# Cross-attention over 64 batches: who makes the output's last step, when x is turned, and the order of both ends

## The chip, the cores and the metric

One core of a Trainium2 chip runs the whole kernel in one launch. The metric is the time of the launch on the device in microseconds (us), as the median of several runs; lower is better. The times of one profiled execution are also used, and they are said to be so.

## What is computed

There are 64 batches. In each, `x` is 256 x 512 and `ctx` 256 x 384, all float32:

```python
text_p  = x   @ W_text  + b_text          # 256 x 512
audio_p = ctx @ W_audio + b_audio         # 256 x 512
Q = layer_norm(text_p,  g1, beta1)
K = layer_norm(audio_p, g2, beta2)
alpha = softmax(Q @ K.T / sqrt(512))      # 256 x 256
H = (alpha @ audio_p) @ W_out + b_out
out = layer_norm(H + x, g_out, beta_out)
```

The last layer norm is, for each row y: subtract the mean, multiply by `g_out` (the "shift"), multiply by the row's 1/sqrt(var + eps), and add `beta_out`. The last two are "the output's last step" below.

## The kernel before, in words

A batch's 256 rows are two tiles of 128 partitions. The instructions of every engine run in the order in which the program writes them down (`tc.manual_schedule()`): no planner moves them, and an instruction that waits holds everything behind it on its engine. Waits between engines come from the tile framework, by the tiles that are read and written. "Turning" is VectorE's 32 x 32 block transpose; rows go to DRAM and come back in blocks of 32 rows (`store`, `fetch`) so that a turn gives a full transpose.

The three products with weights are made with fewer multiplications than usual, by sums of blocks. `Thirds` does k (from ctx, object `k2`) and the output (object `o`, with W_audio and W_out folded into `wao`); its block sums `csum` and `zsum` are seven GpSimd additions each (`Sides.add`). Its products fall into steps `one` to `five` on TensorE in the PSUM places M (`ps_m`), L (`ps_l`), T and U (`ps_u`), N (`ps_n`). Between the steps stand VectorE instructions that read and rewrite PSUM: `after_one` (a copy of N1, then T = N0 - N1), `after_three` (a copy of T, then L0 = M0 + t and L1 = M1 - t), `after_four` (two), and ScalarE/VectorE copies `after_five`, `leave`, `leave_plus`. `Fork` does q from x in two PSUM banks (`ps_f`); its block sums `xsum` are four GpSimd additions, and its VectorE steps are `after_six` (two) and `after_five` (one).

The main loop runs over b from 0 to 61 and is a pipeline. One iteration, "batch b" below, holds: k and q of batch b+2 (`k2`, `q2`); the scores and the softmax of b (`at`); the context product of b-1 (`last`); the output product of b-2 (`old`); and the last layer norm of b-3 (`settled`). The turns in it are `turn_c(b+3)`, `q[b+1].turn()`, `k[b+1].turn([0])` and `([1])`, `turn_x(b+3)`, and `turn_e` of b-1. The layer norm of `settled` is: `sums` and `deviations` on ScalarE (L782, L790), 1/sqrt on GpSimd (L372 and L376, tile `rstd`), and on VectorE `shift` for both tiles (L897) and `settle` for both (L906):

```python
    def settle(self, t):
        nc.vector.scalar_tensor_tensor(
            self.y[:, t, :], self.y[:, t, :], self.r[t], beo_sb, ALU.mult, ALU.add
        )
```

`settle(0)` stands in batch b behind `shift(1)`; `settle(1)` stands in the next iteration, followed by the store of both tiles on SyncE's queue. What follows the loop (batches 61 to 63: `old`, `last`, `at`, `end`) is written out by hand, as is everything ahead of it, where weights are centred, folded and summed.

Of the kernel before, what the change touches and what calls it, by code (L numbers as in the profile page):

```python
# [11 lines left out]
ALU = mybir.AluOpType  # L12
# [10 lines left out]
def kernel(  # L23
# [18 lines left out]
    nc = tc.nc  # L42
# [171 lines left out]
    def bias_parts():  # L214

        part = once.tile([P, D], F32, tag="e", name="part")
        nc.vector.tensor_scalar(part, wo_sb[:, 0, :], bac_sb[:, 0:1], None, ALU.mult)
        for k in range(1, HC):
            nc.vector.scalar_tensor_tensor(
                part, wo_sb[:, k, :], bac_sb[:, k : k + 1], part, ALU.mult, ALU.add  # L220
            )

        nc.vector.tensor_tensor(part[:1], part[:1], bo_sb, ALU.add)
        return part

    wao_sb = const.tile([P, AC, D], F32, tag="wao", name="wao")
    bao_sb = const.tile([P, D], F32, tag="bao", name="bao")
# [54 lines left out]
    def sum_x(xT):  # L282

        n = DC // 2
        part = lambda i, j: xT[:, j * n : (j + 1) * n, bass.ts(i, P)]
        s = work.tile([P, 4, n, P], F32, tag="xsum", name="xsum")
        add = nc.gpsimd.tensor_tensor
        add(s[:, 0], part(1, 0), part(1, 1), ALU.add)
        add(s[:, 1], s[:, 0], part(0, 0), ALU.subtract)
        add(s[:, 2], part(0, 0), part(1, 0), ALU.subtract)  # L290
        add(s[:, 3], part(0, 1), s[:, 1], ALU.subtract)
        ss = {
            1: part(0, 0), 2: part(0, 1), 4: part(1, 1),
            5: s[:, 0], 6: s[:, 1], 7: s[:, 2], 3: s[:, 3],
        }
        return {p: [ap[:, k, :] for k in range(n)] for p, ap in ss.items()}
# [357 lines left out]
    class Attention:  # L654
# [252 lines left out]
                self.y[:, t, :], self.y[:, t, :], self.r[t], beo_sb, ALU.mult, ALU.add  # L907
            )

        def finish(self, lo=0, n=LT):  # L910
            for t in range(lo, lo + n):
                self.shift(t)
                self.settle(t)

        def store(self, lo=0, n=LT):
            nc.sync.dma_start(
# [4 lines left out]
    def turn_x(b):  # L921
        xT = work.tile([P, DC, L], F32, tag="xT", name=f"xT_{b}")
        turn(xT, blocks[b][1], DC)
        return xT

    def turn_c(b):
        cT = work.tile([P, AC, S], F32, tag="cT", name=f"cT_{b}")
        turn(cT, blocks[b][0], AC)
        return cT
# [91 lines left out]
    k[0].turn()  # L1021
    k[0].affine(g2_sb, be2_sb)
    part = bias_parts()
    wa_t = const.tile([P, 11, W3], F32, tag="wa_thirds", name="wa_thirds")
    wa_blocks = third_weights(wa_sb, wa_t, [0])
    fold_multiply(2, 0, 2)
    q[1].six()
    q[1].after_six()
    q[0].turn()
    cT[2] = turn_c(2)  # L1030
    cs[2] = Sides(cT.pop(2), "csum").add()
    fold_multiply(2, 2, 4)
# [2 lines left out]
    q[1].five()  # L1035
    q[1].after_five()
    xT[2] = turn_x(2)
    xs[2] = sum_x(xT.pop(2))
    third_weights(wa_sb, wa_t, [1], nc.vector)
    fold_bias(part)  # L1040
    q[1].rest()
    q[1].square()
    q[1].scales()
    ba_delta = third_bias(ba_sb, "ba_delta")
    bao_delta = third_bias(bao_sb, "bao_delta")
    Thirds.seed_with(ba_sb)
# [13 lines left out]
    for b in range(B - 2):  # L1060
        at = att[b] = att.get(b) or Attention(b)
        settled, old, last = att.pop(b - 3, None), att.get(b - 2), att.get(b - 1)
        three = b + 3 < B
        if b + 4 < B and b != 1:
            load_c(b + 4)
            load_x(b + 4)
        if b == 2:
            go_sb = row(g_out, "go")
            beo_sb = row(beta_out, "beo")
        if b == 0:  # L1070
            at.score(0, 8)
            Fork.seed()
        k2 = k[b + 2] = Thirds("k", b + 2, cs.pop(b + 2), wa_blocks, ba_sb, ba_delta)
        if b < 3:
            q[b + 2] = Fork(b + 2, xs.pop(b + 2), wt_blocks)
        q2 = q[b + 2]
        if settled:
            settled.sums()
        k2.one()
        k2.after_one()  # L1080
        if b < 2:
            Fork.clear()
        if b == 1:
            last.reciprocals()
            last.divide_e()
            last.store_e()
            load_c(b + 4)
            last.fetch_e()
            load_c_rows(b)
            load_x(b + 4)  # L1090
        k2.two()
        if old:
            old.context_two(0)
            old.context_two(1)
            old.copy_two()
        k2.three()
        if three:
            cT[b + 3] = turn_c(b + 3)
        if b:
            at.affine_keys(0, 1)  # L1100
        k2.after_three()
        if old:
            old.start_products()
        if b < 3:
            q2.one()
            q2.after_one()
        q2.seven()
        q2.after_seven()
        if b:
            at.affine_keys(2, 3)  # L1110
        if done:
            done.settle(1)
            done.store()
        done = settled
        if b > 1:
            last.fetch_e()
            load_c_rows(b)
            load_x_rows(b - 1)
        if not three:
            last_rows(B - 2)  # L1120
            last_rows(B - 1)
        q2.six()
        q2.after_six()
        if settled:
            settled.deviations()
        if three:
            cs[b + 3] = Sides(cT.pop(b + 3), "csum").add(2 if b > 1 else 5)
        k2.four()
        k2.after_four()
        if settled:  # L1130
            settled.shift(0)
        q2.five()
        q2.after_five()
        if settled:
            settled.shift(1)
            settled.settle(0)
        if b:
            at.affine_queries(0, 1)
        k2.five()
        k2.after_five()  # L1140
        k2.leave()
        k2.last_middle()
        if three:
            cs[b + 3].add(3 if b > 1 else 0)
        if old:
            old.o.seed()
        elif three:
            k2.seed()
        if b:
            at.affine_queries(2, 3)  # L1150
        q2.rest()
        q2.square()
        q2.scales()
        q[b + 1].turn()
        k[b + 1].turn([0])
        k2.square()
        k2.scales()
        if b:
            at.score(0, 2)
        if old:  # L1160
            old.o.one()
            old.o.after_one()
            old.o.two()
        if three:
            xT[b + 3] = turn_x(b + 3)
        if b:
            at.score(2, 4)
        if old:
            old.o.three()
            old.o.after_three()  # L1170
        k[b + 1].turn([1])
        if b:
            at.score(4, 7)
        if not three:
            att[b + 1] = Attention(b + 1)
            att[b + 1].affine_queries()
        q2.normalise()
        q2.store()
        if old:
            old.o.four()  # L1180
            old.o.after_four()
        if last:
            last.turn_e()
        if b:
            at.score(7, 8)
        if old:
            old.o.five()
        if three:
            Fork.seed()
        k2.normalise()  # L1190
        k2.store()
        q2.fetch()
        k2.fetch()
        if three:
            cs[b + 3].add()
            xs[b + 3] = sum_x(xT.pop(b + 3))
        if b < 2:
            wao_blocks = third_weights(wao_sb, wao_t, [b])
        at.maxima()
        if three and b:  # L1200
            Fork.clear()
        if not three:
            att[b + 1].affine_keys()
        at.exponentials()
        if three and b > 1:
            q3 = q[b + 3] = Fork(b + 3, xs.pop(b + 3), wt_blocks)
            q3.one()
            q3.after_one()
        if old:
            old.o.leave_plus(x_rows[b - 2], at.reciprocals)  # L1210
        elif b:
            at.reciprocals()
        if last:
            last.context_one()
        if three and old:
            k2.seed()
        if b:
            at.divide_e()
        if three and b:
            at.store_e()  # L1220
        if last:
            last.copy_one()

    settled, old, last = att[B - 5], att[B - 4], att[B - 3]
    at = att[B - 2]
    load_x_rows(B - 3)
    done.settle(1)
    done.store()
    for t in range(ST):
        old.context_two(t)  # L1230
# [17 lines left out]
    old.o.three()  # L1248
    old.o.after_three()
    k[B - 1].turn()  # L1250
    q[B - 1].turn()
    for t in range(ST):
        last.context_two(t)
    last.copy_two()
# [2 lines left out]
    k[B - 1].affine(g2_sb, be2_sb)  # L1257
    last.start_products()
    old.o.four()
    settled.settle(0)  # L1260
    old.o.after_four()
    settled.settle(1)
    settled.store()
    old.o.five()
# [15 lines left out]
    end.score(0, 8)  # L1280
    old.shift(0)
    old.shift(1)
    at.evict(0)
    at.scales(0, 1)
    last.o.four()
    last.o.after_four()
    end.maxima()
    end.exponentials()
    old.settle(0)
    old.settle(1)  # L1290
    old.store()
# [2 lines left out]
    at.settle(0)  # L1294
    last.o.five()
    last.o.leave_plus(x_rows[B - 3], lambda: None)
    at.multiply(1, bank[4])
    at.evict(1)
    at.scale_soon(1)
    end.transpose_e(bank[5])  # L1300
    end.copy_e()
    last.statistics()
    end.context()
    at.shift(1)
    at.settle_beside(1)
    at.store()
# [50 lines left out]
```

## Time and profile before

| | |
|---|---|
| median of 3 runs | 1411.28 us (1408.72 to 1413.8) |
| the profiled execution's own time | 1412.36 us |
| its span, first to last instruction | 1410.6 us |
| busy: TensorE, its weight loads | 98%, 88% |
| busy: VectorE, ScalarE, GpSimd | 87%, 78%, 72% |
| mean granted TensorE clock | 0.995 |
| one iteration of the loop in its middle | 21.2 us |

Engines are named PE (TensorE), PEld (its weight loads), DVE (VectorE), ACT (ScalarE), POOL (GpSimd) and SP (SyncE, which issues the DMAs). A timeline line gives the start in us from the first instruction, the duration, the engine, the line in the source, the operation, out<-in by tile names, the shape, how many instructions were merged, and in brackets how long the engine had been idle and what ended that. A matmul is recorded twice, and its end is modelled, so the distance from one start to the next is the better measure of what a matmul costs.

### The profile page before, as it was taken

Reading aid. Unit: us, or ns where it says so; the run is one execution under the profiler, and the core shown is the slowest. Engines: PE = TensorE matmul, PEld = TensorE weight load, DVE = VectorE, ACT = ScalarE, POOL = GpSimd, SP = SyncE. Lnnn points to the kernel's source line nnn. Section 1 sums busy time; section 2 is a strip of 40 time slices with the busy share of each in tenths; the row PEclk is TensorE's granted clock in tenths of the full one; section 3 lists DMA queues with packets and bytes.
Section 4 is the critical chain, followed back from the end, with each engine's and each line's share of the span. In section 5 each row is a group of like instructions: output and inputs, shape, how many; then the busy total and the mean of one; then the engine's idle time right before and its main releaser. Section 6 shows DMA issues by size and latency. Waiting matters only on the chain.

```text
span 1410.6 us, 26095 instructions
## 1 busy us (share of the span) xinstructions
PE 1388.2 (98%) x7423; PEld 1241.4 (88%) x7423; DVE 1225.0 (87%) x2559; ACT 1094.5 (78%) x2815; POOL 1017.5 (72%) x1685
## 2 busy tenths in 40 slices
PE   9899999999999999999999999999999999999996
PEld 5689999999999999999999999999999999999874
DVE  5768988988988988888988989988988988988877
ACT  4678878878878877877877878877877877877873
POOL 4787777777777777777777777787787687687644
PEclk9999999999999999999999999999999999999999
DMA  9688878778777878788778788887877778788661
GB/s 219 168 245 239 233 232 245 224 243 242 225 241 237 235 235 246 222 241 239 229 242 244 228 234 245 230 235 231 239 240 230 244 235 241 231 233 237 207 204 62
DMA packets 449095, 322.00 MB, mean 228 GB/s; under 512 B 153782, under 2 KB 381622, under 8 KB 448951
## 3 DMA queue, kind: packets, MB, share of 16 engines
q1 hardware_dynamic: 448854, 320.20, 77.9%
q8 instruction: 60, 0.98, 0.3%
q14 instruction: 85, 0.69, 0.2%
q10 hardware_dynamic: 96, 0.13, 0.0%
HBM read 203.57 MB, written 116.65 MB: 227 GB/s over the span
## 4 chain that ended last, share of the span: by engine, by line
PE 91%; DVE 2%; ACT 2%; POOL 2%; issue 1%; DMA 1%; SPq 1%; DVEq 0%; ACTq 0%; POOLq 0%
PE ps_f L603 26%; PE ps_m L502 16%; PE ps_sc L672 14%; PE ps_z L738 11%; PE ps_n L502 10%; PE ps_u L502 7%; PE ps_l L502 5%; SPq L72 1%; POOL csum L320 0%; DMA eq<-ed 0%; PE ps_f L392 0%; ACT qr L652 0%; POOL zsum L320 0%; PE ps_m L807 0%; ACT qT L477 0%
## 5 line engine op out<-in xcount | busy, mean ns | idle before, releaser
L320 POOL TENSOR_TENSOR zsum<-zT 128x256 f32<-128x256 f32 x124 | 73.6, 594 | 271.4 <-ACT zT L756 264.6
L672 PE MATMUL ps_sc<-kT,qT 128*128 128x256 f32 x1024 | 262.6, 381 | 0.5 <-ACT zT L753 0.5
L320 POOL TENSOR_TENSOR zsum<-zsum,zT 128x256 f32<-128x256 f32 x310 | 215.8, 714 | 14.6
L672 PEld LDWEIGHTS ps_sc<-kT,qT 128*128 128x128 f32 x1024 | 187.6, 191 | 18.5 <-ACT zT L753 0.9
L320 POOL TENSOR_TENSOR csum<-csum,cT 128x256 f32<-128x256 f32 x310 | 192.0, 628 | 10.0
L603 PE MATMUL ps_f<-wtsum,xsum 128*128 128x256 f32 x756 | 189.9, 387 | 1.7 <-DVE ps_f L486 1.4
L906 DVE SCALAR_TENSOR_TENSOR yr<-yr,rstd,beo 128x512 f32<-128x512 f32 x124 | 144.1, 1163 | 51.8 <-POOL rstd L376 51.8
L738 PE MATMUL ps_z<-eT,c 128*128 128x256 f32 x768 | 186.6, 379 | 1.9 <-ACT e L689 1.2
L738 PEld LDWEIGHTS ps_z<-eT,c 128*128 128x128 f32 x768 | 142.9, 190 | 19.1 <-ACT e L689 1.6
L603 PEld LDWEIGHTS ps_f<-wtsum,xsum 128*128 128x128 f32 x756 | 136.1, 190 | 22.2 <-DVE ps_f L486 2.2
L376 POOL TENSOR_TENSOR rstd<-ve,nhalf 128x2 f32<-128x2 f32 x192 | 136.3, 710 | 16.0
L477 ACT ACTIVATE qT<-qT,columns 128x256 f32<-128x256 f32 x256 | 138.8, 592 | 1.7 <-DVE qT L75 1.7
L477 ACT ACTIVATE kT<-kT,columns 128x256 f32<-128x256 f32 x256 | 139.7, 597 | 0.4 <-DVE kT L75 0.4
L603 PE MATMUL ps_f<-wt,xT 128*128 128x256 f32 x504 | 130.3, 381 | 1.4 <-ACT ps_f L595 1.4
L897 DVE SCALAR_TENSOR_TENSOR yr<-yr,nm,go 128x512 f32<-128x512 f32 x124 | 117.4, 949 | 0.0
L561 ACT COPY kr<-ps_l 128x344 f32<-128x344 f32 x62 | 27.6, 446 | 100.5 <-DVE kr L486 100.2
L603 PEld LDWEIGHTS ps_f<-wt,xT 128*128 128x128 f32 x504 | 93.5, 191 | 11.8 <-ACT ps_f L595 1.6
L689 ACT ACTIVATE e<-ps_sc,nmx 128x256 f32<-128x256 f32 x128 | 59.4, 469 | 55.9 <-DVE nmx L682 55.9
L486 DVE TENSOR_TENSOR ps_l<-ps_m,t 128x172 f32<-128x172 f32 x248 | 85.7, 346 | 17.2 <-DVE t L543 0.5
L790 ACT ACTIVATE junk<-yr,nm 128x512 f32<-128x512 f32 x124 | 87.9, 712 | 0.0
L652 ACT ACTIVATE qr<-ps_f,rstd 128x512 f32<-128x512 f32 x126 | 79.7, 683 | 6.1 <-POOL rstd L376 6.1
L438 ACT ACTIVATE kr<-kr,rstd 128x512 f32<-128x512 f32 x126 | 84.1, 720 | 0.0
(227 smaller groups left out, 3712.6 us busy)
## 6 DMA issues: line engine op xcount, KB each, us to landing
kd<-kr SPq DMA_DIRECT2D x64, 512.0 KB, 2.8
kq<-kd SPq DMA_DIRECT2D x256, 128.0 KB, 3.2
qd<-qr SPq DMA_DIRECT2D x64, 512.0 KB, 2.8
qq<-qd SPq DMA_DIRECT2D x256, 128.0 KB, 2.7
xq<-in_x_dram SPq DMA_DIRECT2D x252, 128.0 KB, 3.3
x<-in_x_dram SPq DMA_DIRECT2D x63, 512.0 KB, 4.8
out_dram<-yr SPq DMA_DIRECT2D x62, 512.0 KB, 3.9
cq<-in_ctx_dram SPq DMA_DIRECT2D x252, 96.0 KB, 3.5
```

Of the source, the lines that this page charges most:

```text
L320: nc.gpsimd.tensor_tensor(*step)
L376: nc.gpsimd.tensor_tensor(r, ve, nhalf[:, :n], ALU.pow)
L438: nc.scalar.mul(row, row, self.r[t])
L477: nc.scalar.activation(self.T[:, k, :], self.T[:, k, :], AF.Identity, bias=bet[:, k : k + 1], scale=gam[:, k : k + 1],)
L486: nc.vector.tensor_tensor(o, i0, i1, op)
L502: nc.tensor.matmul(place, lhsT=self.sides.of[n], rhs=self.weights[n], start=(n == 14), stop=True, skip_group_check=True,)
L603: nc.tensor.matmul(place, lhsT=side, rhs=w, start=False, stop=True, skip_group_check=True)
L672: nc.tensor.matmul(self.sc[:, t, :], lhsT=self.qT[:, k, bass.ts(t, P)], rhs=self.kT[:, k, :], start=(k == 0), stop=(k == HC - 1),)
L738: nc.tensor.matmul(ps, lhsT=c_rows[self.b][:, s, bass.ts(j, P)], rhs=self.eT[:, s, :], start=(s == 0), stop=(s == ST - 1),)
L790: nc.scalar.activation(junk, self.y[:, t, :], AF.Square, bias=self.nm[:, t : t + 1], accum_out=self.ssq[:, t : t + 1],)
L897: nc.vector.scalar_tensor_tensor(row, row, self.nm[:, t : t + 1], go_sb, ALU.add, ALU.mult)
L906: nc.vector.scalar_tensor_tensor(self.y[:, t, :], self.y[:, t, :], self.r[t], beo_sb, ALU.mult, ALU.add)
```

## The change

The last step of the output is split. In the loop, `scale_row` multiplies by 1/sqrt on ScalarE and `lift_rows` adds `beta_out` for both tiles on GpSimd at the end of the same iteration; the store waits for that. `settle` on VectorE is left for the batches behind the loop. `turn_x(b+3)` moves ahead of the output's `after_one`, and `k[b+1].turn([1])` ahead of its `after_three`. Ahead of the loop, the bias product `part` is made in pieces around `q[1]`'s steps, `sum_x` for batch 2 goes behind q[1]'s scales, and in iteration 0 all seven block sums of ctx are made at once. In the last iteration `affine_keys` goes behind the exponentials and `copy_one`, and behind the loop `after_four`, `maxima`, `exponentials` and `transpose_e` go ahead of neighbours.

```diff
         nc.vector.tensor_scalar(part, wo_sb[:, 0, :], bac_sb[:, 0:1], None, ALU.mult)
-        for k in range(1, HC):
+        return part
+
+    def bias_rest(part, lo, n):
+
+        for k in range(lo, n):
             nc.vector.scalar_tensor_tensor(
                 part, wo_sb[:, k, :], bac_sb[:, k : k + 1], part, ALU.mult, ALU.add
             )
 
-        nc.vector.tensor_tensor(part[:1], part[:1], bo_sb, ALU.add)
-        return part
+        if n == HC:
+            nc.vector.tensor_tensor(part[:1], part[:1], bo_sb, ALU.add)
...
-        def finish(self, lo=0, n=LT):
-            for t in range(lo, lo + n):
-                self.shift(t)
-                self.settle(t)
+        def scale_row(self, t):
+            nc.scalar.mul(self.y[:, t, :], self.y[:, t, :], self.r[t])
+
+        def lift_rows(self):
+            for t in range(LT):
+                nc.gpsimd.tensor_tensor(self.y[:, t, :], self.y[:, t, :], beo_sb, ALU.add)
...
     part = bias_parts()
+    bias_rest(part, 1, 2)
     wa_t = const.tile([P, 11, W3], F32, tag="wa_thirds", name="wa_thirds")
     wa_blocks = third_weights(wa_sb, wa_t, [0])
     fold_multiply(2, 0, 2)
     q[1].six()
     q[1].after_six()
     q[0].turn()
+    bias_rest(part, 2, HC)
     cT[2] = turn_c(2)
...
     xT[2] = turn_x(2)
-    xs[2] = sum_x(xT.pop(2))
     third_weights(wa_sb, wa_t, [1], nc.vector)
     fold_bias(part)
     q[1].rest()
     q[1].square()
     q[1].scales()
+    xs[2] = sum_x(xT.pop(2))
...
         if done:
-            done.settle(1)
             done.store()
...
         if three:
-            cs[b + 3] = Sides(cT.pop(b + 3), "csum").add(2 if b > 1 else 5)
+            cs[b + 3] = Sides(cT.pop(b + 3), "csum").add(2 if b > 1 else 7)
         k2.four()
         k2.after_four()
...
         if settled:
             settled.shift(1)
-            settled.settle(0)
         if b:
             at.affine_queries(0, 1)
         k2.five()
         k2.after_five()
+        if settled:
+            settled.scale_row(0)
         k2.leave()
...
         if b:
             at.affine_queries(2, 3)
+        if settled:
+            settled.scale_row(1)
         q2.rest()
         q2.square()
         q2.scales()
         q[b + 1].turn()
         k[b + 1].turn([0])
+        if three:
+            xT[b + 3] = turn_x(b + 3)
         k2.square()
...
             old.o.one()
             old.o.after_one()
             old.o.two()
-        if three:
-            xT[b + 3] = turn_x(b + 3)
+        k[b + 1].turn([1])
         if b:
             at.score(2, 4)
         if old:
             old.o.three()
             old.o.after_three()
-        k[b + 1].turn([1])
...
         if three:
             cs[b + 3].add()
             xs[b + 3] = sum_x(xT.pop(b + 3))
+        if settled:
+            settled.lift_rows()
...
         at.maxima()
         if three and b:
             Fork.clear()
-        if not three:
-            att[b + 1].affine_keys()
         at.exponentials()
...
         if last:
             last.copy_one()
+        if not three:
+            att[b + 1].affine_keys()
...
     load_x_rows(B - 3)
-    done.settle(1)
     done.store()
...
     k[B - 1].turn()
-    q[B - 1].turn()
...
     old.o.four()
+    old.o.after_four()
+    q[B - 1].turn()
     settled.settle(0)
-    old.o.after_four()
     settled.settle(1)
...
     old.shift(0)
     old.shift(1)
+    end.maxima()
+    end.exponentials()
+    last.o.four()
+    last.o.after_four()
     at.evict(0)
     at.scales(0, 1)
-    last.o.four()
-    last.o.after_four()
-    end.maxima()
-    end.exponentials()
     old.settle(0)
...
     last.o.leave_plus(x_rows[B - 3], lambda: None)
+    end.transpose_e(bank[5])
+    end.copy_e()
     at.multiply(1, bank[4])
     at.evict(1)
     at.scale_soon(1)
-    end.transpose_e(bank[5])
-    end.copy_e()
+    end.context()
     last.statistics()
-    end.context()
```

## The prediction

> **What bounds the kernel now.** I read the page first: its busy line, and the first lines of its chain that ended last.
>
> ```profile
> PE 1388.2 (98%) x7423; PEld 1241.4 (88%) x7423; DVE 1225.0 (87%) x2559; ACT 1094.5 (78%) x2815; POOL 1017.5 (72%) x1685
> PE 91%; DVE 2%; ACT 2%; POOL 2%; issue 1%; DMA 1%; SPq 1%; DVEq 0%; ACTq 0%; POOLq 0%
> ```
>
> TensorE carries the chain, so work taken off VectorE is worth only what it takes out of TensorE's order. Busy time does not show short waits, because a matmul's end is modelled; distances from start to start do. In the loop a record of 256 columns costs 0.216 us and one of 172 columns 0.146 (median distances). A batch has 56 and 60 of them (scores 16, context 12, q 28; k 30, output 30): 56 x 0.216 + 60 x 0.146 = 20.86 us. The windows view of one period, and the same from the batch at 804.75, say 21.2. So 0.35 us of each batch is waiting. The timeline of TensorE shows where:
>
> ```profile
> 810.25 1.11 PE L603 MATMUL ps_f<-wtsum,xsum 128*128 128x256 f32 x4
> ...
> 819.75 0.45 PE L502 MATMUL ps_u<-wao_thirds,zsum 128*128 128x172 f32 x2
> 820.19 0.85 PE L502 MATMUL ps_m<-wao_thirds,zsum 128*128 128x172 f32 x4
> ```
>
> Two ps_u records should end in a start at 819.75 + 0.29 = 820.04; ps_m starts at 820.19, 0.15 late. Its group of four takes 0.85 where the same group takes 0.75 without a wait: 0.10 more, since its weights were not loaded ahead. The group at 810.25 (`q2.five`) takes 1.11 where others of its shape take 1.03: 0.09. Together 0.34. VectorE's timeline says what they waited for:
>
> ```profile
> 808.35 1.16 DVE L906 SCALAR_TENSOR_TENSOR yr<-yr,rstd,beo 128x512 f32<-128x512 f32 x1
> 809.43 0.42 DVE L486 TENSOR_TENSOR ps_f<-ps_f,s 128x256 f32<-128x256 f32 x1
> 809.76 0.42 DVE L486 TENSOR_TENSOR ps_f<-ps_f,bt_step 128x256 f32<-128x256 f32 x1
> ...
> 813.73 1.20 DVE L906 SCALAR_TENSOR_TENSOR yr<-yr,rstd,beo 128x512 f32<-128x512 f32 x1 [0.87 <-POOL rstd L376]
> ...
> 817.85 1.23 DVE L75 STREAM_TRANSPOSE xT<-xq 128x1024 f32<-128x1024 f32 x1
> 819.01 0.30 DVE L543 COPY t<-ps_u 128x172 f32<-128x172 f32 x1
> 819.41 0.72 DVE L486 TENSOR_TENSOR ps_l<-ps_m,t 128x172 f32<-128x172 f32 x2
> ```
>
> `settle(1)` at 808.35 pushes `after_six` so far that it ends at 810.18, and `q2.five` needs it. `settle(0)` costs 0.87 of waiting and 1.12 of work; behind it all turns are late, and `after_three`, which could have read T at 818.65 (TensorE's `o.three` ends there), starts at 819.01 and ends at 820.13.
>
> **The steady batches.** Without `settle(1)`, `after_six` is bound by `q2.six`, whose product ends at 808.96: it ends near 809.75, 0.43 earlier, and `q2.five` loses no time. Without `settle(0)`, VectorE goes on as soon as ScalarE has copied n (813.51): two additions to about 814.15, qT 1.16 to 815.3, half of kT 0.59 to 815.9, xT 1.16 to 817.05 (now here), `after_one` 0.6 to 817.65 (it needs `o.one`, done at 816.86; `o.three` needs it at 818.1), the other half of kT 0.65 to 818.3. So VectorE is free when `o.three` ends. Batch 2 has no `settled` and shows that case in the trace of before: its `after_three` (98.03, 0.72 us) ends at 98.75, and
>
> ```profile
> 98.68 0.46 PE L502 MATMUL ps_u<-wao_thirds,zsum 128*128 128x172 f32 x2
> 98.97 0.75 PE L502 MATMUL ps_m<-wao_thirds,zsum 128*128 128x172 f32 x4
> ```
>
> ps_m starts 0.29 behind ps_u and takes 0.75: no wait. Gain 0.34 for each of batches 4 to 60, 57 x 0.34 = 19.4 us.
>
> What is added has to find room. ScalarE: `scale_row` costs 0.61 to 0.72 (the row scaling at L843 took 0.72, a pair at L438 1.33). `scale_row(0)` waits for `rstd` (813.69), and behind it are queued `leave`, the seed of M, `affine_queries(2, 3)`, `scale_row(1)` and the squares. Before, `leave` itself waited until 815.21:
>
> ```profile
> 815.21 0.45 ACT L561 COPY kr<-ps_l 128x344 f32<-128x344 f32 x1 [1.70 <-DVE kr L486]
> ```
>
> Now it waits for additions that are done at 814.2. `scale_row(0)` 813.73 to 814.4, `leave` to 814.85, seed to 815.25, affine to 816.3, 0.8 earlier than before (817.11; the score products need it at 817.28), `scale_row(1)` to 816.95: the squares start where they did (817.01). Cost nothing; the cover is the 1.70. GpSimd: two additions of 128x512. The same one at L844 took 1.26, those of `add_bias` (L934) 1.5 each, so 2.5 to 3.0, in a gap of 4.34:
>
> ```profile
> 807.42 0.73 POOL L320 TENSOR_TENSOR zsum<-zT 128x256 f32<-128x256 f32 x1 [4.34 <-ACT zT L756]
> ```
>
> They start at 803.2 and end by 806.2. VectorE's work beside them is `leave_plus`, which reads PSUM; its 344-column additions took 0.52 both beside GpSimd's sums and after them, so I charge nothing. The store moves from VectorE's `settle(1)` to `lift_rows`, one iteration earlier; on SyncE's queue it issued at 811.00 straight behind the x loads, so nothing behind it (eq, c and x loads) moves. Limits for the steady part: the full 0.34 (19.4), and half of it if a new wait of 0.17 comes up (9.7). I take the full one, being the batch 2 row.
>
> [...]
>
> **Ahead of the loop.** Before, `q[1].five` started 1.52 late at 40.65 (`after_six` behind `part`), and q[2].one at 52.82, 1.38 idle, for the seed behind `q[1].normalise`, which waited for `rstd` behind `sum_x`. Now `after_six` starts when `q[1].six` is done (37.6), 0.5 after VectorE is free; that idle half microsecond stays in VectorE's order, `part` is whole at 42.2 instead of 39.9, and `fold_bias` waits from 40.0 to 42.2; `after_five` and with it `q[1].rest` come 0.45 later than before (43.5). Then `rstd` is ready at 48.4 instead of 51.2, the 1.38 and its 0.15 vanish, and q[2].one starts at 51.64: 1.2 gained. The 2.35 in front of 65.56 (`csum`) stays nearly whole: making seven sums at once frees GpSimd, but `after_one` still ends at 65.35. That stretch hangs on ScalarE, busy from 59.5 to 70.3, so the gain passes through unchanged. One thing can spoil it: the granted clock.
>
> ```profile
> 1355.90:1359.30 3.40, 1.72 (x7) 1.15 (x7) 2.02 (x7) 3.17 (x10) 0.20 (x1) 1.00 0.81 255
> 1359.30:1362.70 3.40, 3.40 (x9) 2.65 (x9) 1.08 (x2) 2.78 (x9) 3.16 (x6) 0.50 0.98 200
> ```
>
> Behind 3.4 us in which TensorE (second column after the length) was busy 1.72 or less, the clock is 0.50 for 3.4 us; 2.04 busy at 38.3 to 41.7 had no such effect. The new wait of 2.2 at 40 may be such a stretch, and half speed costs 1.7. I take even odds: gain 1.2 - 0.85, about 0.4; bounds 0.5 lost, 1.3 gained.
>
> [...] The three stretches at 0.50 here are 3.4 long. [...]
>
> **Behind the loop.** Batches 60 and 61 wait for `after_one` behind two whole turns (0.48 and 0.32); batch 61's goes, with smaller ones: 0.8 in all (I count 60's small ones above). In batch 61 four `affine_keys` (2.07) stand before the exponentials:
>
> ```profile
> 1357.19 1.13 PE L738 MATMUL ps_z<-eT,c 128*128 128x256 f32 x4 [1.21 <-ACT e L689]
> ...
> 1372.55 0.85 PE L502 MATMUL ps_m<-wao_thirds,zT 128*128 128x172 f32 x4 [1.38 <-DVE ps_u L486]
> ...
> 1396.20 4.54 PE L807 MATMUL ps_m<-wao,zT 128*128 128x512 f32 x6 [2.23 <-ACT zT L753]
> ```
>
> Exponentials first: the 1.21, the 0.48 behind it and the half-speed stretch (1.8) go, 2.7 at the end of the scores; but `copy_two` now stands behind `affine_keys` at the old place, `zsum` starts as before, and its first five steps (3.5) hold `o.one` back: 1.4 remain. `after_four` ahead of q's turn: the 1.38 goes (1.5 with the late weights), but the next `o.one` then waits 0.8 for `zsum`: 0.7 to 0.8 remain. `end.maxima` and the transposes earlier: the last product's 2.23 and its half-speed stretch go, and VectorE, without a pause from 1380, is late next with `last.settle` at 1399.5; `end.evict(0)` waited until 1400.78, so 1.2 remain. Sum 0.8 + 1.4 + 0.8 + 1.2 = 4.2; bounds 1.5 and 5.5.
>
> **Sum.** 19.4 + 0.4 + 4.2 = 24.0 less: span 1386.6, the profiled execution 1412.36 - 24.0 = 1388.4. The median of before lies 1.1 under that execution: 1387.3.
>
> **Rivals.** First, a new wait takes half: `after_one` now stands behind xT and has 0.45 to spare. If the turns run 0.5 to 0.7 longer or start that much later, `o.three` waits 0.1 to 0.2 a batch: 6 to 11 back, 1393 to 1399. For it: five VectorE instructions now lie between n's copy and `after_one`. Against it: turns of 1.16 and 0.59 in every batch. Second, no change: TensorE's 0.15 is its own latency behind `o.three`, not VectorE's queue; then only the ends move, 1407 to 1411. Against it: batch 2. Third, slower: `lift_rows` overruns. It decides at about 5 us for the pair (4.2 of room until zT comes, 0.8 that `affine_queries` has won); beyond that each microsecond goes through `zsum`, `rstd`, `scale_row(0)`, `leave` and `affine_queries` into every score product. A 256-column sum at 1371.33 took 1.13 beside VectorE's settles; two adds at 3 us would cost 1 x 57, less the other gains 1411 + 57 - 24 = 1444. Against it: 1.26 and 1.5.
>
> **How the numbers follow.** Forecast 0.74 (its own range 1383.5 to 1392), half 0.15, no change 0.05, slower 0.06. The range 1383.5 to 1400 takes in the forecast and the first rival. Faster by more than 0.3% (4.2 us, about what a measurement of this kernel can tell from no change) holds in the first two cases: 0.88; the second rival 0.06 with the edges; slower 0.06.
>
> **What would show it.** A period of 20.86 to 20.9; L906 gone from the loop; ps_m of `o.four` 0.29 behind ps_u; GpSimd's pair inside 803 to 806; `leave` earlier on ScalarE. Wrong, if a wait stands in front of ps_u (`o.three`) or the score products, or if zsum's idle time is gone.

## The result, and the profile after

The changed kernel takes 1387.24 us (median of 4 runs, 1386.56 to 1388.19) against 1411.97 us for the kernel before beside it (4 runs): a ratio of 0.9828, 95% interval 0.9808 to 0.9847. The profiled execution took 1388.19 us, its span is 1386.4 us. Lines move by four: settle is L910, shift L901, the Fork's product L607, the Thirds' product L506.

The page after: the busy line, the first line of the chain that ended last, and two groups (columns: instructions, busy us and mean ns, idle before).

```profile
PE 1364.5 (98%) x7423; PEld 1245.0 (90%) x7423; DVE 1113.4 (80%) x2441; ACT 1163.5 (84%) x2933; POOL 1126.4 (81%) x1803
...
PE 95%; DVE 2%; ACT 1%; issue 0%; POOL 0%; DMA 0%; DVEq 0%; SPq 0%; ACTq 0%; POOLq 0%
...
L919 POOL TENSOR_TENSOR yr<-yr,beo 128x512 f32<-128x512 f32 x118 | 148.0, 1278 | 0.0
...
L901 DVE SCALAR_TENSOR_TENSOR yr<-yr,nm,go 128x512 f32<-128x512 f32 x124 | 103.6, 837 | 0.0
```

VectorE lost 111.6 us of work, ScalarE and GpSimd gained 69.0 and 108.9, and the time fell by 24: what counts is not the sum but which waits went. TensorE's share of the chain rose from 91% to 95%. The shift on VectorE fell from 949 to 837 ns, though nothing in it was changed.

Where the time went in the two profiled executions is read from the starts of `k2.one`, the first product of a batch, in the two traces (us from the span's start; the period is the mean from batch 4 to 60):

| | batch 0 | batch 4 | batch 60 | batch 61 | span's end | period |
|---|---|---|---|---|---|---|
| before | 49.19 | 126.18 | 1313.65 | 1335.38 | 1410.57 | 21.205 |
| after | 50.65 | 127.00 | 1293.86 | 1314.84 | 1386.40 | 20.837 |

So 0.82 was lost ahead of batch 4, 56 x 0.368 = 20.61 was gained up to batch 60, 0.75 in batch 60, and 3.62 from batch 61 on: 24.16 in all.

A steady batch of after, TensorE's timeline (`q2.five`, then `o.three` at 807.09 and `o.four` with its ps_u and ps_m):

```profile
799.28 1.03 PE L607 MATMUL ps_f<-wtsum,xsum 128*128 128x256 f32 x4
...
807.09 0.46 PE L506 MATMUL ps_u<-wao_thirds,zsum 128*128 128x172 f32 x2
...
808.67 0.46 PE L506 MATMUL ps_u<-wao_thirds,zsum 128*128 128x172 f32 x2
808.97 0.75 PE L506 MATMUL ps_m<-wao_thirds,zsum 128*128 128x172 f32 x4
```

All three waits of before are gone: `q2.five` takes 1.03 (was 1.11), ps_m starts 0.30 behind ps_u (was 0.44) and takes 0.75 (was 0.85). VectorE in the same batch:

```profile
805.84 0.34 DVE L542 COPY n<-ps_n 128x172 f32<-128x172 f32 x1
806.21 0.34 DVE L490 TENSOR_TENSOR ps_u<-ps_n,n 128x172 f32<-128x172 f32 x1
...
807.58 0.34 DVE L547 COPY t<-ps_u 128x172 f32<-128x172 f32 x1 [0.41 <-PE ps_u L506]
808.02 0.73 DVE L490 TENSOR_TENSOR ps_l<-ps_m,t 128x172 f32<-128x172 f32 x2
```

The bracket is the point: VectorE now stands idle for 0.41 in front of `after_three`, until TensorE's `o.three` ends, where before TensorE waited for VectorE. What was added, on ScalarE and then on GpSimd:

```profile
802.44 0.72 ACT L915 ACTIVATE yr<-yr,rstd 128x512 f32<-128x512 f32 x1
803.07 0.42 ACT L565 COPY kr<-ps_l 128x344 f32<-128x344 f32 x1
```

```profile
812.61 2.51 POOL L919 TENSOR_TENSOR yr<-yr,beo 128x512 f32<-128x512 f32 x2
817.29 0.73 POOL L324 TENSOR_TENSOR zsum<-zT 128x256 f32<-128x256 f32 x1 [2.18 <-ACT zT L760]
```

`scale_row(0)` starts without idle time, and `leave`, which had stood for 1.70, follows it at once. `lift_rows` takes 2.51 out of GpSimd's gap in front of `zsum`, which shrinks from 4.34 to 2.18.

Ahead of the loop, and behind it (TensorE's timeline):

```profile
41.71 1.15 PE L250 MATMUL ps_n<-part,ones 128*128 128x512 f32 x2 [2.20 <-DVE part L228]
43.01 2.05 PE L607 MATMUL ps_f<-wt,xsum 128*128 128x256 f32 x4 [0.16 <-DVE ps_f L490]
...
65.31 0.53 PE L506 MATMUL ps_u<-wa_thirds,csum 128*128 128x172 f32 x2 [2.29 <-DVE ps_u L490]
```

```profile
1336.32 3.90 PE L676 MATMUL ps_sc<-kT,qT 128*128 128x256 f32 x16 [0.48 <-ACT kT L481]
1340.99 0.97 PE L506 MATMUL ps_n<-wao,zsum 128*128 128x172 f32 x4 [0.34 <-POOL zsum L324]
...
1352.57 0.82 PE L506 MATMUL ps_n<-wao,zsum 128*128 128x172 f32 x4 [1.20 <-DVE yr L490]
...
1368.84 2.84 PE L811 MATMUL ps_m<-wao,zT 128*128 128x512 f32 x6
```

In front, `fold_bias` waits 2.20 for the rest of `part`, as forecast, and the four products behind it take 2.05 where 1.03 is their price: the granted clock is 0.50 from 42.68 to 46.09, and again from 66.57 to 73.40. (It is 0.50 from 1377.29 to the end as well, but TensorE's last matmul ends at 1374.27.) Behind the loop the waits of 1.21, 1.38 and 2.23 are gone, but a wait of 1.20 for VectorE's `leave_plus` is new.

### The profile page after: what moved, and what is told of

It reads as the page before. It is cut to its first block, busy times and chain, and to the rows that moved or that the text cites. A ratio compares the mean times of both kernels' runs of the same rounds, so it can differ in the third digit from the quotient of the medians.

```text
span 1386.4 us, 26272 instructions
## 1 busy us (share of the span) xinstructions
PE 1364.5 (98%) x7423; PEld 1245.0 (90%) x7423; DVE 1113.4 (80%) x2441; ACT 1163.5 (84%) x2933; POOL 1126.4 (81%) x1803
## 4 chain that ended last, share of the span: by engine, by line
PE 95%; DVE 2%; ACT 1%; issue 0%; POOL 0%; DMA 0%; DVEq 0%; SPq 0%; ACTq 0%; POOLq 0%
PE ps_f L607 28%; PE ps_sc L676 15%; PE ps_m L506 15%; PE ps_z L742 11%; PE ps_n L506 10%; PE ps_u L506 8%; PE ps_l L506 5%; DVE yr L910 0%; PE ps_f L396 0%; DMA c<-in_ctx_dram 0%; PE ps_l L236 0%; PE ps_m L236 0%; PE ps_n L396 0%; PE ps_u L396 0%; ACT kT L481 0%
## 5 line engine op out<-in xcount | busy, mean ns | idle before, releaser
L324 POOL TENSOR_TENSOR zsum<-zsum,zT 128x256 f32<-128x256 f32 x310 | 197.1, 653 | 14.6
L607 PE MATMUL ps_f<-wtsum,xsum 128*128 128x256 f32 x756 | 186.4, 382 | 1.1 <-ACT ps_f L618 0.6
L324 POOL TENSOR_TENSOR csum<-csum,cT 128x256 f32<-128x256 f32 x310 | 173.3, 568 | 10.0
L607 PEld LDWEIGHTS ps_f<-wtsum,xsum 128*128 128x128 f32 x756 | 139.0, 191 | 16.8 <-ACT ps_f L618 1.7
L919 POOL TENSOR_TENSOR yr<-yr,beo 128x512 f32<-128x512 f32 x118 | 148.0, 1278 | 0.0
L607 PE MATMUL ps_f<-wt,xT 128*128 128x256 f32 x504 | 130.0, 380 | 0.0
L901 DVE SCALAR_TENSOR_TENSOR yr<-yr,nm,go 128x512 f32<-128x512 f32 x124 | 103.6, 837 | 0.0
L607 PEld LDWEIGHTS ps_f<-wt,xT 128*128 128x128 f32 x504 | 93.5, 191 | 10.3 <-issue 0.3
L490 DVE TENSOR_TENSOR ps_f<-ps_f,s 128x256 f32<-128x256 f32 x126 | 54.5, 432 | 48.4 <-PE ps_f L607 45.4
L915 ACT ACTIVATE yr<-yr,rstd 128x512 f32<-128x512 f32 x118 | 84.5, 716 | 0.0
```

The source lines that it names most:

```text
L324: nc.gpsimd.tensor_tensor(*step)
L490: nc.vector.tensor_tensor(o, i0, i1, op)
L607: nc.tensor.matmul(place, lhsT=side, rhs=w, start=False, stop=True, skip_group_check=True)
L901: nc.vector.scalar_tensor_tensor(row, row, self.nm[:, t : t + 1], go_sb, ALU.add, ALU.mult)
L915: nc.scalar.mul(self.y[:, t, :], self.y[:, t, :], self.r[t])
L919: nc.gpsimd.tensor_tensor(self.y[:, t, :], self.y[:, t, :], beo_sb, ALU.add)
```

## The experiments

The theory: the steady gain comes from VectorE's `settle` leaving VectorE's order, in two parts (`settle(1)` holds `q2.five`, `settle(0)` holds `o.three` and `o.four`); the moved turns bring nothing by themselves; the ends bring a little. The rivals: the moved turns do the work; the ends do; GpSimd is nearer to its limit than thought.

**The loop's part alone.** Ends as before, the split in, and `turn_x(b+3)` and `k[b+1].turn([1])` at their new places.

```diff
-            settled.settle(0)
+            settled.scale_row(0)          # behind k2.after_five
...
+            settled.scale_row(1)          # behind affine_queries(2, 3)
+            settled.lift_rows()           # behind sum_x
-            done.settle(1)
```

> Only the loop's edits (last step split over ScalarE and GpSimd, both turns moved); both ends as before. Theory (settle in VectorE's queue made TensorE wait 0.34 to 0.37 us in each batch): batches 4 to 60 take 20.84 us each as in the changed kernel, the half-speed stretch near 43 us is gone, the old tail is back: 1387.2 - 0.8 + 3.1 = about 1389.5. Rival (the ends carry much of the gain): 1395 or more.

Measured: 1388.98 us (4 runs, 1386.82 to 1389.57) against 1409.92, ratio 0.9846 (0.9831 to 0.9861); period 20.837. The loop alone has the whole gain of each batch.

**The split alone.** The turns stay at their old places. Against the loop's part alone:

```diff
         k[b + 1].turn([0])
-        if three:
-            xT[b + 3] = turn_x(b + 3)
...
             old.o.two()
-        k[b + 1].turn([1])
+        if three:
+            xT[b + 3] = turn_x(b + 3)
...
             old.o.after_three()
+        k[b + 1].turn([1])
```

> Only the split of the last step; the turns and both ends as before. Theory: the turns' move is worth nothing, since without settle(0) VectorE reaches after_three just as o.three ends, as in batch 2 of the kernel before: within 3 us of e1_loop, 1389 to 1393, ps_m of o.four 0.29 to 0.35 behind ps_u. Rival (the gain needs x turned ahead of the output's first sum): the 0.25 us wait at ps_m stays, 1389.5 + 57 x 0.25 = about 1404.

Measured: 1389.02 us (4 runs, 1387.42 to 1391.08), ratio 0.985 (0.9834 to 0.9866); period 20.837, the same to the third decimal. The moved turns are worth nothing in the steady batches: with `settle` gone, VectorE has room in either order.

**The moved turns alone.** `settle` stays on VectorE. Against before:

```diff
         k[b + 1].turn([0])
+        if three:
+            xT[b + 3] = turn_x(b + 3)
...
             old.o.two()
-        if three:
-            xT[b + 3] = turn_x(b + 3)
+        k[b + 1].turn([1])
...
             old.o.after_three()
-        k[b + 1].turn([1])
```

> Only the two turns moved; settle stays on VectorE, both ends as before. Theory: behind settle(0) the x turn pushes after_one to about 819.0 in the frame of the kernel before, where o.three needs it at 818.1: a new wait of 0.95 us at ps_u (o.three), the 0.25 at ps_m gone, net +0.7 to 0.8 us a batch, 1411 + 57 x 0.75 = about 1454. Rival (turning x early is what frees after_three): 1411 - 57 x 0.25 = about 1397.

Measured: 1460.64 us (4 runs, 1459.7 to 1463.43), ratio 1.036 (1.0344 to 1.0377), period 22.088. TensorE's waits (us in total, times, longest) and one of them in its timeline:

```profile
PE ps_u L502 <- DVE ps_u L486: 54.0, 58, 1.5
```

```profile
805.98 0.53 PE L502 MATMUL ps_u<-wao_thirds,zsum 128*128 128x172 f32 x2 [0.93 <-DVE ps_u L486]
```

`o.three` waits 0.93 in every batch for an `after_one` that now stands behind xT's turn. This is the prediction's first rival, and it is real: it needs `settle(0)` in front of the turns to come true. The 1.12 of work and 0.87 of waiting that the split takes away are what gives `after_one` its room. A batch costs 0.88 more than before, where 0.75 was expected.

**The ends alone.** The loop is as before; all edits ahead of the loop, in its last iteration and behind it are in. Some of them:

```diff
+    bias_rest(part, 1, 2)                 # the rest behind q[0].turn
+    xs[2] = sum_x(xT.pop(2))              # behind q[1].scales
...
-            att[b + 1].affine_keys()      # ahead of at.exponentials
+            att[b + 1].affine_keys()      # behind last.copy_one
```

> Only the two ends reordered; the loop as before. Theory: ahead of the loop 0.8 us lost (2.2 us wait for the bias product, half speed behind it), behind it 3.1 gained: about 1409, the period stays 21.2. Rival (the front's edits gain as predicted, 0.4 to 1.2): 1406.5 to 1408.

Measured: 1410.41 us (10 runs, 1407.13 to 1411.21), ratio 0.9998 (0.9988 to 1.0007). The trace has the two halves: batch 4 starts at 127.62, 1.44 later than before; from batch 61 to the end it takes 71.89 instead of 75.18. By the two traces 1.8 us should be left as a gain; the runs show nothing that can be told from no change. One reason can be read off the mean granted clock, which falls with every stretch at half speed: it is 0.995 in the profiled execution of before, and 0.996 or 0.997 in 12 of the 13 executions of before that were timed beside this run.

**The old front in the changed kernel.**

```diff
-    return part
+    for k in range(1, HC):                # part whole, ahead of q[1].six
...
+    xs[2] = sum_x(xT.pop(2))              # behind turn_x(2), as before
...
-            cs[b + 3] = Sides(cT.pop(b + 3), "csum").add(2 if b > 1 else 7)
+            cs[b + 3] = Sides(cT.pop(b + 3), "csum").add(2 if b > 1 else 5)
```

> The changed kernel with the old order ahead of the loop (part in one piece ahead of q[1]'s after_six, sum_x ahead of the scales, five sums of ctx at first). Theory, from the run with the loop alone: the new front costs 1.35 us (batch 4 starts at 127.00 in the changed kernel, at 125.65 with the loop alone), so this one lands at 1387.2 - 1.35 = about 1385.9, with batch 4 at 125.6 to 125.7. Rival, the prediction's own term: the new front gains 0.4, so this one takes 1387.6 and batch 4 starts later than 127.0.

Measured: 1388.51 us (5 runs, 1386.93 to 1389.04), ratio 0.9831 (0.9818 to 0.9845). Batch 4 starts at 126.21 in its trace, 0.79 ahead of the changed kernel's, yet the median is not lower. A difference of one microsecond in front is below what these runs resolve; the traces have to carry it.

**q[1].five ahead of the rest of the bias product.** The candidate for a better front.

```diff
     q[0].turn()
-    bias_rest(part, 2, HC)
...
     q[1].after_five()
+    bias_rest(part, 2, HC)
...
-    fold_bias(part)
     q[1].rest()
+    fold_bias(part)
```

> The changed kernel with q[1].five, after_five and rest ahead of the rest of part and of fold_bias. Theory: TensorE's 2.20 us of waiting for part at 39.5 goes, and with it the half-speed stretch that follows at 42.7; batch 0 starts near 47.5 instead of 50.65, and if that passes through, the time is 1384 to 1385. Rival: what follows hangs on other engines' chains (sums of x and ctx on GpSimd, normalisation on ScalarE), which swallow it by batch 4: batch 4 still at 126.5 to 127.0, 1386.5 to 1387.2.

Measured: 1386.24 us (4 runs, 1384.76 to 1388.96), ratio 0.9819 (0.9805 to 0.9832). TensorE's timeline:

```profile
40.59 1.10 PE L607 MATMUL ps_f<-wt,xsum 128*128 128x256 f32 x4 [0.62 <-POOL wa_thirds L340]
...
43.25 1.02 PE L250 MATMUL ps_n<-part,ones 128*128 128x512 f32 x2
```

`fold_bias` waits for nothing, there is no stretch at half speed before 65, batch 0 starts at 47.56, 3.09 earlier than in the changed kernel, and batch 4 at 125.44, 1.56 earlier. So about half passes through: less than the theory had, more than the rival. Run beside each other once more on one chip:

> The changed kernel itself once more, as the measure for the next one on the same chip: 1387.2, batch 0 at 50.5 to 51.3 and, as in three of the four profiles with this front, a half-speed stretch at about 43.

> The kernel with q[1].five, after_five and rest ahead of the rest of part and of fold_bias, once more. Theory: 1.0 to 1.6 less than the changed kernel on the same chip (its batch 4 started 1.56 earlier), 1385.7 to 1386.2, and no half-speed stretch before 60. Rival: the difference seen was scatter between runs: both within 0.3.

Measured: the changed kernel 1388.10 us (5 runs, 1385.87 to 1389.86), ratio 0.9826 (0.9811 to 0.9841); the new front 1386.78 (4 runs, 1386.58 to 1387.80), ratio 0.9824 (0.9811 to 0.9838). Batch 4 starts at 128.63 and 125.81. In both pairs of traces the new order reaches batch 4 earlier, but the times do not separate: it is shown that the wait goes, not that the kernel is faster.

**settle(1) back on VectorE.** Tile 0 stays with ScalarE and GpSimd.

```diff
+            done.settle(1)                # old place, ahead of done.store
...
-            settled.scale_row(1)
-            for t in range(LT):           # in lift_rows
+            for t in range(1):
```

> The changed kernel with tile 1 finished by VectorE's settle(1) at its old place, tile 0 still by ScalarE and GpSimd. Theory: settle(1) delays after_six by 0.43 and q2.five by 0.09 a batch, 57 x 0.09 = 5.1: about 1392.4, period 20.93. Rival 1: q2.five's late start had another cause, no change: 1387.2. Rival 2: settle(1) pushes more than that one step: 0.2 a batch or more, over 1398.

Measured: 1394.06 us (4 runs, 1391.37 to 1394.78), ratio 0.9868 (0.9855 to 0.9882); period 20.923, 0.086 more. VectorE's and TensorE's timelines in one batch:

```profile
798.55 1.16 DVE L910 SCALAR_TENSOR_TENSOR yr<-yr,rstd,beo 128x512 f32<-128x512 f32 x1
799.63 0.42 DVE L490 TENSOR_TENSOR ps_f<-ps_f,s 128x256 f32<-128x256 f32 x1
799.97 0.42 DVE L490 TENSOR_TENSOR ps_f<-ps_f,bt_step 128x256 f32<-128x256 f32 x1
```

```profile
800.46 1.11 PE L607 MATMUL ps_f<-wtsum,xsum 128*128 128x256 f32 x4
```

The 1.11 of before is back; no other start in TensorE's loop is later than in after. The median is 6.8 above the changed kernel's, of which the period gives 57 x 0.086 = 4.9; the other 1.9 are less than these runs scatter. So `settle(1)` accounts for 0.086 of the 0.368, and by subtraction `settle(0)` for the rest, 0.282; `settle(0)` was not put back by itself.

**lift_rows with four and with six additions.** Beta is added, subtracted and added again, which leaves the sum as it was but for rounding. Four: tile 0 only.

```diff
-                nc.gpsimd.tensor_tensor(self.y[:, t, :], self.y[:, t, :], beo_sb, ALU.add)
+                for op in (ALU.add, ALU.subtract, ALU.add)[: 1 if t else 3]:
+                    nc.gpsimd.tensor_tensor(self.y[:, t, :], self.y[:, t, :], beo_sb, op)
```

> The changed kernel with four GpSimd additions instead of two in lift_rows (tile 0: plus beta, minus beta, plus beta). The pair of 2.5 us becomes some 5.0. Theory of the prediction: 5 us is the point from which it decides (zsum's idle time left is 2.18, affine_queries on ScalarE has won 0.8), so the period moves by 0 to 0.2 us: 1387 to 1398. Rival: GpSimd is then busy 20.0 of 20.8 us, its other waits do not shrink, and most of the 2.5 goes through: more than 1 us a batch, 1444 or more.

Measured: 1410.86 us (10 runs, 1409.1 to 1413.13), ratio 0.9996 (0.9987 to 1.0005); period 21.206, 0.37 more than after (21.23 from batch 7 on). Neither number was hit: less than the rival's 1, more than the theory's 0.2. GpSimd, ScalarE and TensorE:

```profile
827.22 5.21 POOL L920 TENSOR_TENSOR yr<-yr,beo 128x512 f32<-128x512 f32 x4
832.39 0.73 POOL L324 TENSOR_TENSOR zsum<-zT 128x256 f32<-128x256 f32 x1
```

```profile
817.03 0.72 ACT L915 ACTIVATE yr<-yr,rstd 128x512 f32<-128x512 f32 x1 [2.01 <-POOL rstd L380]
817.66 0.42 ACT L565 COPY kr<-ps_l 128x344 f32<-128x344 f32 x1
817.99 0.45 ACT L520 COPY ps_m<-bao 128x344 f32<-128x344 f32 x1
```

```profile
817.62 0.75 PE L506 MATMUL ps_n<-wao,zsum 128*128 128x172 f32 x4
818.49 0.85 PE L506 MATMUL ps_m<-wao,zsum 128*128 128x172 f32 x4
```

The bracket in front of `zsum` is gone: GpSimd no longer waits there. The delay goes through `zsum`, `rstd`, `scale_row(0)` (2.01 of waiting) and `leave` to the seed of M at 817.99, and `o.one`'s M, due at 817.62 + 4 x 0.146 = 818.20, starts at 818.49. Over the loop this wait is 0.26 a batch and the late weight load behind it 0.10. Six additions (both tiles three):

> The changed kernel with six GpSimd additions instead of two in lift_rows (each tile plus, minus, plus beta). Four of them took 5.21 us and cost 0.37 a batch. Theory: GpSimd's order is now a ring without slack (lift_rows, zsum, rstd, scale_row(0) and leave and the seed of M on ScalarE, TensorE's M), so the 2.6 us of two more additions go through whole: 0.37 + 2.6 = 3.0 a batch, period 23.8, about 1387 + 57 x 3.0 = 1558. Rival: the pair had already begun to run beside what it waits for, and only a part, say half, goes through: period 22.5, 1480.

Measured: 1575.73 us (2 runs), ratio 1.1161 (1.1139 to 1.1184); the median period is 24.04. TensorE's waits and GpSimd's timeline:

```profile
PE ps_m L506 <- ACT ps_m L520: 125.8, 55, 2.8
```

```profile
871.39 7.93 POOL L920 TENSOR_TENSOR yr<-yr,beo 128x512 f32<-128x512 f32 x6
879.27 1.19 POOL L324 TENSOR_TENSOR zsum<-zT 128x256 f32<-128x256 f32 x1
```

From four to six the additions grew by 7.93 - 5.21 = 2.72 and the median period by 24.04 - 21.23 = 2.81: all of it goes through, as the ring predicts. The 1558 expected was short of 1575.73, since the period is 24.04 and not 23.8 (57 x 0.24 = 14) and the part from batch 61 on takes 76.44 instead of 71.56. Stretches at half speed also come every 48 us over much of the loop (mean granted clock 0.968 against 0.993), but they cost next to nothing: batches there alternate between 22.45 and 25.72, 24.09 in the mean, and batches without a stretch take 24.04. While GpSimd sets the pace, a slower TensorE seems only to use up its own waiting.

## Why the prediction was right, and where it was not

**The steady batches: right, a little low.** Forecast 0.34 a batch, measured 0.368. Added up over the loop of before, the late starts are 0.146 a batch for ps_m, 0.102 for the late weights behind it and 0.085 for `q2.five`, the three terms of the prediction (0.15, 0.10, 0.09); small ones that it did not count make the rest. The run with `settle(1)` put back prices the third term alone, at 0.086. The run with the split alone shows that nothing else in the change was needed for it. Batch 2 was the right witness: it showed VectorE's order without `settle`.

**The first rival: not here, but near.** With the split `after_one` ends at 806.55 for an `o.three` at 807.09: 0.54 to spare, 0.45 forecast. Without the split the same move costs 0.88 a batch. The split alone has the same period, so this part of the change could have been left out.

**The third rival: its mechanism and its point were right.** It was to decide at about 5 us for the pair. 5.21 costs 0.37 and 7.93 costs 24.04 - 20.84 = 3.20, so it decides at 5.21 - 0.37 = 4.8 by the one and 4.7 by the other. Only the place differs: the first victim is `o.one`'s M behind its seed, which stands ahead of `affine_queries` on ScalarE, not the score products.

**Ahead of the loop: the term failed.** Forecast 0.4 gained, bounds 0.5 lost and 1.3 gained; measured 0.82 lost, and 1.47 if both are counted from `q[1].one`, which happened to start 0.65 earlier in after. From the start of `q[1].one` to batch 4 the time is 93.07 in before, and 92.56 to 93.27 in the three other traces with the old front and the split. The new front takes 91.55 in the one profile without a stretch at half speed at 43 (the run with `settle(1)` put back), 1.5 less, near the 1.2 forecast without that stretch; 94.54, 94.35 and 95.49 in three with it (changed kernel, ends alone, changed kernel again). The two runs with more additions share this front and have the stretch too, so it came in five of six: even odds look too kind.

Above all the term was mis-sized. The prediction charged 1.7 for one stretch, and the front with it takes 2.8 to 3.9 more than the front without: the stretch of before at 65.62, 3.4 us long, came back 6.8 us long at 66.57, which no step of the prediction had looked at. Whether the first stretch comes goes with where the wait of 2.2 falls, and with the wait gone (`q[1].five` first, two traces) it does not come. The windows view on the 3.41 us steps at which the clock changed (after the length: TensorE's busy time; the clock stands after the five engines), first of the changed kernel, then of the run with `settle(1)` put back:

```profile
39.27:42.68 3.41, 1.21 (x4) 0.30 (x2) 3.34 (x5) 2.11 (x5) 1.82 (x3) 1.00 0.77 201
```

```profile
38.64:42.06 3.42, 2.35 (x8) 1.14 (x6) 3.37 (x5) 3.42 (x8) 3.18 (x6) 1.00 0.95 271
42.06:45.47 3.41, 2.16 (x7) 1.26 (x8) 3.38 (x6) 1.72 (x4) 2.70 (x4) 1.00 0.87 228
```

The same wait lies within one step in the first and across two in the second; only the first is followed by half speed. TensorE was not idle in that step, but busy for 1.21 of 3.41 us.

**Behind the loop: the sum was right, for another reason.** Batches 60 and later were to give 0.34 + 4.2 = 4.5 and gave 0.75 + 3.62 = 4.37. But the parts were mis-sized. The wait of 1.38 went and 1.20 came in its place, so `after_four`'s 0.8 is 0.06 (from `o.one` to the next `o.one` 11.64 before, 11.58 after). The scores gave 2.5 instead of 1.4 (from the context product at 1354.10 in before, 1333.09 in after, to `o.one`: 10.38 and 7.90), since `zsum` came only 0.34 late. Above all, most of it is the clock, which the prediction took as certain: it counted both stretches as gone with their waits. The run with the split alone has the old ends with all their waits:

```profile
1334.98 1.13 PE L738 MATMUL ps_z<-eT,c 128*128 128x256 f32 x4 [1.21 <-ACT e L689]
1336.59 3.72 PE L672 MATMUL ps_sc<-kT,qT 128*128 128x256 f32 x16 [0.48 <-ACT zT L753]
...
1372.34 2.84 PE L807 MATMUL ps_m<-wao,zT 128*128 128x512 f32 x6 [2.26 <-ACT zT L753]
```

The scores take 3.72 (5.41 in before) and the last product 2.84 (4.54 in before): the waits are there, the stretches at half speed are not. From batch 61 to the end this run takes 71.99 us; with one stretch (loop alone) 73.25, with two (before) 75.18; the new ends, without one while TensorE still works, 71.42 to 71.89. So the new order by itself is worth 0.1 to 0.6, and about 3 of the 3.62 are the two stretches in the profiled execution of before. They are neither certain nor rare with the old ends: the four traces with them have two, one, none and one (before, loop, split and turns alone). The seven traces with the new ends and at most two additions have none, so the new order does seem to keep them away; with four additions one is back, at 1360.55, with six none behind the loop. Over whole executions the mean granted clock tells the same: the 37 further timings of before in the experiments lie at 0.994 to 0.998, and take 1414.0 us in the mean at the one end and 1409.7 at the other.

The miss in front (1.2), the surplus in the loop (20.61 instead of 56 x 0.34 = 19.0) and 0.2 behind it nearly cancel, and so the forecast of 1387.3 met 1387.24 closer than its steps deserve. The steady 19.4 was earned; the last microsecond is luck.

## What to carry to other kernels

An operation that is taken off a busy engine is worth what it delays in that engine's order, and a batch that happens to lack it shows that price beforehand; the 2.5 us of GpSimd work and 1.4 of ScalarE work were free because both lay in measured gaps in front of a wait. Moving work ahead of a step that another engine waits for needs room made first: the same turns cost 0.88 us a batch without the split and nothing with it. A term of one or two microseconds that hangs on the granted clock should be priced in whole stretches with both outcomes, not at half.

## What was not expected of the hardware

- The stretches at half speed in the traces of before and after start at multiples of one length from each other: in before at 65.62, 1359.27 and 1396.81 (379 and 11 times 3.413 us), in after at 42.68, 66.57 and 1377.29 (7 and 384 times). Whether one came went with how long TensorE was busy in the step of that length in front of it; no step had to be idle. Before has 1.06, 1.73 and 1.18 us ahead of these, and 2.05 (from 38.31) and 2.03 (from 1369.51) ahead of full clock; after has 1.21 and 1.26 ahead of its first two. Elsewhere it was 1.27 (loop alone), 1.12 (`settle(1)` back), 1.47 (`q[1].five` first) and 1.58 (changed kernel again) with a stretch behind it, and 2.35 and 2.16 (`settle(1)` back) without. The split alone has 1.48 from 61.33 to 64.74 and full clock behind it, so these times give no sharp line. The stretch of after at 66.57, in which TensorE was itself busy for 2.33 us, was followed by a second; the one at 42.68 (3.25) and that of before at 65.62 (3.41) were not. The same lines have them in one trace and not in another, as the old ends above show (5.41 and 3.72 us for the scores).
- VectorE's `settle` and GpSimd's additions take longer beside each other in these traces. `settle` takes 1.16 and 1.20 us beside them in a batch of before (808.35 and 813.73), 1.163 in the mean of 124, and 0.75 in its last run (1405.84), with no such addition beside it. The first of the five additions into `csum`, beside `settle(0)` in before and without it in after:

```profile
814.46 1.06 POOL L320 TENSOR_TENSOR csum<-csum,cT 128x256 f32<-128x256 f32 x1
```

```profile
803.18 0.74 POOL L324 TENSOR_TENSOR csum<-csum,cT 128x256 f32<-128x256 f32 x1
```

In the mean the five fell from 628 to 568 ns, the same of `zsum` from 714 to 653, and VectorE's shift from 949 to 837. The run with `settle(1)` back tells them apart: `zsum` is back at 713 and the shift at 954, `csum` stays at 569, so the first two belong to `settle(1)` and the last to `settle(0)`. What the cause is, no run shows.
